# L0 attention: the maxima's bias on VectorE, the exponentials one slot earlier, the projection's bias as a product on TensorE

## The chip, the cores and the metric

The kernel runs on one core of a Trainium2 chip. The metric is the device time of one execution in microseconds. In the profile PE is TensorE, ACT is ScalarE, DVE is VectorE, POOL is GpSimd and SP is SyncE, which issues most of the DMAs. Each of them works through its own instructions in order.

## The reference

The program is a stack of six layers on x of 8 x 512 x 256, all in float32:

```python
x = x + 0.5 * _L0_ffn_ref(_layernorm(x), ...)    # f1: 64 experts, top 3
x = x + _L0_attn_ref(_layernorm(x), ...)         # a1: the layer that is changed
x = x + 0.5 * _L0_ffn_ref(_layernorm(x), ...)    # f2
x = x + 0.5 * _L1_ffn_ref(_layernorm(x), ...)    # f3: 8 experts, top 2
x = x + _L1_attn_ref(_layernorm(x), ...)         # a2
x = x + 0.5 * _L1_ffn_ref(_layernorm(x), ...)    # f4
```

The changed layer, for each batch row of 512 tokens, 16 heads and a window of 32 earlier tokens:

```python
strain = disp_win - disp[:, :, :, None, :]
bond_act = gelu(strain @ w_strain + b_strain + state[:, :, :, None, :] @ w_state_i
                + state_win @ w_state_j + rel_emb @ w_pos)
bond_logits = (bond_act @ w_bond_out)[..., 0] + b_bond_out[0]
damage_act = gelu(strain @ w_damage + b_damage)
damage = sigmoid((damage_act @ w_damage_out)[..., 0] + b_damage_out[0])
logits = where(cmask, bond_logits - damage * 10.0, -inf)
weights = softmax(logits, axis=-1)
out = einsum('bntd,bntde->bnte', weights, val_win)
return out.transpose(0, 2, 1, 3).reshape(Bx, Tx, Cx) @ w_cproj + b_cproj
```

## The kernel before

A batch row is 4 tiles of 128 tokens (`NT`). `l0_attn` cuts the gelus of a batch row into 16 units: 2 groups of 8 heads, 2 halves of the window, and 4 interleaved offsets in each. One unit is 4 offsets x 512 tokens on 128 partitions, once for the bond (tile `ub`) and once for the damage (tile `ud`).

The order of the work is written out by hand. Time is counted in slots, one unit to a slot, 16 slots to a batch row, 8 batch rows. In slot s:

- `unit_add(s)` adds up the arguments of unit s: `ub` by four instructions on DVE (L670), `ud` by one long one on POOL (L676);
- `unit_act(s-1)` runs both gelus of the unit before on ACT (L681);
- then come the evacuations (`later`) of what the steps of slot s-1 left in PSUM;
- `unit_pe(s-2)` reduces the unit before that on PE (L692);
- and last the steps that the list `plan` has for this slot. A step's PE part is issued at once, the function that it returns is run in the next slot.

`ub` and `ud` have three buffers each, so unit s can be added up once PE is done with unit s-3. Four PSUM banks hold the sums of the units, two `bq`, and the two banks of pool `ps` (tile `m`) serve every other product in turn.

The steps of `plan` that matter here, with their slot counted from the batch row's first unit (the steps of later and earlier batch rows share these slots: k and k - 16 or k + 16 coincide):

- 6, 10, 14, 18 `logits`: the tanh of a half on ACT (`th`, L701), then one instruction on DVE (L702);
- 11, 12 and 19, 20 `less_maxima`: PE turns logits into tokens by partitions (L717, L721); in the next slot DVE takes the maximum of each head's window (`mx`, L729), ACT adds the constant `b_bond` to the maxima (L730), and DVE writes logits + `b_bond` - `mx` into `e` (L731). `e` has a single buffer, which holds a whole batch row;
- 22 `exponentials`: one instruction on ACT over all of `e` (L740); 22 `fetch_values`;
- 23, 24 `weights`: DVE sums `e` (L746) and takes the reciprocal, POOL multiplies (L748), and 8 DMAs for each half write the result into a band in DRAM (L753);
- 23 to 34 `fetch_weights`, `turn_weights`: the band is read back and turned; 33, 37 `weigh`: it is multiplied with the values, and ACT copies the result to `o` (L802);
- 39, 41 `project`: `o` times `w_cproj` on PE (L812), and DVE adds it to `x` (L816);
- for the batch row that comes after: -14 `norm`, -13 and -12 `turn` (L558, copied by ACT to `xnT` at L559), -12 `add_bias`, which adds `b_cproj` to the whole `x` of the batch row on POOL (L550), -11 and -10 `means`, -10 to 2 the keys and queries, of which `damage_keys` leaves `dk` on ACT (L657) and `dq` on DVE (L658).

For the first 132 slots each engine keeps exactly this order of issue. The slots after that, the end of the last batch row, are ordered together with the routing of the next layer by the tile framework.

Of the kernel before, what the change touches and what calls it, by code (L numbers as in the profile page):

```python
# [8 lines left out]
F32 = mybir.dt.float32  # L9
I32 = mybir.dt.int32  # L10
U32 = mybir.dt.uint32
AF = mybir.ActivationFunctionType
ALU = mybir.AluOpType
# [4 lines left out]
P = 128  # L18
NB = 8
T = 512  # L20
D = 256
NT = T // P
KC = D // P
# [20 lines left out]
def bcast_rows(ap, n):  # L44

    return bass.AP(tensor=ap.tensor, offset=ap.offset, ap=[[0, n]] + [list(d) for d in ap.ap[1:]])
# [295 lines left out]
def l0_attn(c, w, tag):  # L342
    nc, tc = c.nc, c.tc
    with ExitStack() as ctx:
        dram = ctx.enter_context(tc.tile_pool(name=f"{tag}_dram", bufs=1, space=DRAM))
        const = ctx.enter_context(tc.tile_pool(name=f"{tag}_const", bufs=1))
# [21 lines left out]
        w_cproj = const.tile([P, KC, D], F32, name="w_cproj")  # L368
# [3 lines left out]
            nc.sync.dma_start(b_disp, w["b_disp"].rearrange("o (g p) -> p (o g)", p=P))  # L372
        b_val = const.tile([P, D], F32, name="b_val")
        nc.sync.dma_start(b_val, bcast_rows(w["b_val"], P))
        b_cproj = const.tile([P, D], F32, name="b_cproj")
        nc.sync.dma_start(b_cproj, bcast_rows(w["b_cproj"], P))
        b_bond = const.tile([P, 1], F32, name="b_bond")
        nc.sync.dma_start(b_bond, bcast_rows(w["b_bond_out"], P))
        b_dam = const.tile([P, 1], F32, name="b_dam")
# [159 lines left out]
        def norm(b):  # L539
# [5 lines left out]
            row[b] = {  # L545
                "xn": xn, "xnT": rp.tile([P, KC, T], F32, name="xnT"), "zT": rp.tile([P, KC, T], F32, name="zT")
            }

        def add_bias(b):
            nc.gpsimd.tensor_tensor(  # L550
                c.x[b], c.x[b], b_cproj.unsqueeze(1).to_broadcast([P, NT, D]), ALU.add
            )

        def turn(b, kc):
            xn = row[b]["xn"]
# [151 lines left out]
        def less_maxima(b, g, i2):  # L707
            t = grp[b, g]
            if g == 0 and i2 == 0:
                row[b]["e"] = rp.tile([P, NT, 2, GH, WIN], F32, name="e")  # L710
            tp = ps.tile([P, T], F32, name="m")
            tv = tp.rearrange("p (i h a d) -> p i h a d", i=2, h=GH, a=2)
            for j in range(2):
                i = 2 * i2 + j
                for half in range(2):
                    if i == 0:
                        nc.tensor.matmul(  # L717
                            tv[:, j, :, half, :], lhsT=c.ident, rhs=mask[:, :, 16 * half : 16 * (half + 1)],
                            start=True, stop=False,
                        )  # L720
                    nc.tensor.matmul(  # L721
                        tv[:, j, :, half, :], lhsT=t["lo", half][:, i * P : (i + 1) * P], rhs=place,
                        start=(i > 0), stop=True,
                    )

            def after():
                mx = sp.tile([P, 2, GH], F32, name="mx")
                tw = tp.rearrange("p (i h d) -> p i h d", i=2, h=GH)
                nc.vector.tensor_reduce(out=mx, in_=tw, axis=AX.X, op=ALU.max)  # L729
                nc.scalar.activation(mx, mx, AF.Identity, bias=b_bond)  # L730
                nc.vector.scalar_tensor_tensor(  # L731
                    out=row[b]["e"][:, 2 * i2 : 2 * i2 + 2, g], in0=tw, scalar=b_bond,
                    in1=mx.unsqueeze(3).to_broadcast([P, 2, GH, WIN]), op0=ALU.add, op1=ALU.subtract,
                )

            return after
# [70 lines left out]
        def project(b, i2):  # L807
            o = row[b].pop(("o", i2))
            mm = ps.tile([P, 2, D], F32, name="m")
            for j in range(2):  # L810
                for a in range(KC):
                    nc.tensor.matmul(  # L812
                        mm[:, j, :], lhsT=o[:, j, a, :], rhs=w_cproj[:, a, :], start=(a == 0), stop=(a == KC - 1)
                    )
            xs = c.x[b][:, 2 * i2 : 2 * i2 + 2, :]
            return lambda: nc.vector.tensor_tensor(xs, xs, mm, ALU.add)  # L816


        plan = [
            (-14, norm), (-13, turn, 0), (-12, turn, 1), (-12, add_bias), (-11, means, 0), (-10, means, 1),  # L820
            (-10, disp, 0), (-9, values, 0), (-8, values, 1), (-8, state, 0), (-7, disp, 1), (-6, bond_keys, 0),
            (-5, bond_queries, 0), (-4, damage_keys, 0), (-3, state, 1), (0, bond_keys, 1), (1, bond_queries, 1),
            (2, damage_keys, 1), (6, logits, 0, 0), (10, logits, 0, 1), (11, less_maxima, 0, 0),
            (12, less_maxima, 0, 1), (14, logits, 1, 0), (18, logits, 1, 1), (19, less_maxima, 1, 0),
            (20, less_maxima, 1, 1), (22, exponentials), (22, fetch_values), (23, weights, 0), (24, weights, 1),
            (24, fetch_weights, 0), (24, fetch_weights, 1), (25, fetch_weights, 2), (29, turn_weights, 0, 0),
            (30, turn_weights, 0, 1), (30, turn_weights, 1, 0), (31, fetch_weights, 3), (31, turn_weights, 1, 1),
            (31, turn_weights, 2, 0), (32, turn_weights, 2, 1), (33, weigh, 0), (33, turn_weights, 3, 0),
            (34, turn_weights, 3, 1), (37, weigh, 1), (39, project, 0), (41, project, 1),
        ]  # L830
        slots = {}
# [1090 lines left out]
def macaron_kernel(ctx, tc, x, l0a, l0f, l1a, l1f, out):  # L1922
# [10 lines left out]
    with ExitStack() as k0:  # L1933
        k0_ = l0_consts(c, l0f, k0.enter_context(c.tc.tile_pool(name="l0_const", bufs=1, side="right")))
        c.zero = k0_.zero
        f1, f2 = (l0_ffn(c, l0f, tag, k0_, l0_dram) for tag in ("f1", "f2"))
        a1 = l0_attn(c, l0a, "a1")
        next(a1)
        with c.tc.tile_pool(name="f1_w", bufs=5) as wp:
            f1.route(2, lambda: next(a1))  # L1940
            next(a1)
            f1.experts(wp)
        next(a1)
        f2.route(1)
        next(a1, None)
        consts, load = l1_ffn_consts(c, l1f, ctx.enter_context(c.tc.tile_pool(name="f_const", bufs=1)))
        with c.tc.tile_pool(name="f2_w", bufs=5) as wp:
            f2.experts(wp, load)
# [176 lines left out]
```

## Time and profile before

| what | value |
|---|---|
| time, median of 3 runs | 3248.82 us (3236.14 to 3258.5) |
| the profiled execution | 3218.18 us, of which the span is 3216.4 us |
| PE, PEld, DVE, ACT, POOL busy in the span | 87%, 62%, 50%, 51%, 52% |
| mean granted TensorE clock | 0.92 |
| busy in 640 to 1313 us: PE, DVE, ACT, POOL | 559.33, 491.10, 592.68, 573.11 of 673 us |
| gelus L681 (`ub`, `ud`), 128 each | 1920 and 1914 ns |
| `ud` on POOL L676, 128 | 4195 ns |
| `ub` on DVE L670, 512 | 738 ns |
| maxima's bias on ACT L730, 32 | 305 ns |
| projection's bias on POOL L550, 8 | 2368 ns |
| exponentials on ACT L740, 8 | 1913 ns |
| table loads on ACT, each | 1283 ns |

The shares of the whole span are means over six layers with different limits. L0 attention has the stretch from about 650 to 1400 us; in its steady part, the 128 slots, a batch row repeats nearly the same timeline. A line of the timeline has the start, the duration, the engine, the line of the source, the operation, the tiles it writes and reads, the shape and a count; in brackets it has the idle time before it and what ended that. A count over 1 means several instructions in a row, and the duration is theirs together.

### The profile page before, as it was taken

The page shows a single profiled execution, that of the slowest core. Times are in us where ns is not written, and L with a number is a line of the kernel's source. Part 1 is how long each engine was busy: PE and PEld are TensorE (multiplying, and loading weights), DVE is VectorE, ACT ScalarE, POOL GpSimd, SP SyncE. Part 2 cuts the span into 40 slices and gives each one's busy share as a digit, 9 for nine tenths or more (in the row PEclk, how much of TensorE's full clock was granted, in tenths as well). Part 3 has the DMA queues.
Part 4 walks back from the last instruction along what each step waited for, and adds up shares of the span by engine and source line. Part 5 has one row for each costly group of instructions (what it writes and reads, how often), then busy time and mean ns, then how long its engine had stood idle before and what let it go on. Part 6 is the DMA issues. An engine that isn't in the chain of part 4 may idle for free. (4 is left out here: it accounts for less than half of the span.)

```text
span 3216.4 us, 53865 instructions
## 1 busy us (share of the span) xinstructions
PE 2784.4 (87%) x20353; PEld 1997.6 (62%) x20353; DVE 1593.0 (50%) x3773; ACT 1641.3 (51%) x2608; POOL 1658.6 (52%) x1298
## 2 busy tenths in 40 slices
PE   6699999978888888778999997787899999998783
PEld 6688888833334343467888896575455555554662
DVE  7511111167777777672111113675657666573564
ACT  4133333369999999632333333266444535434452
POOL 3344444368888888524444442255535454324565
PEclk9799999988999999788999997799889989898897
DMA  7599999531555666786999994144101010001355
GB/s 232 192 304 306 306 302 307 171 104 10 78 85 85 84 85 88 84 240 215 307 308 304 303 307 132 40 141 130 29 15 41 28 35 27 20 7 58 109 172 162
DMA packets 378178, 478.66 MB, mean 149 GB/s; under 512 B 93080, under 2 KB 339872, under 8 KB 361536
## 3 DMA queue, kind: packets, MB, share of 16 engines
q1 hardware_dynamic: 339376, 403.50, 44.3%
q0 software_dynamic: 38544, 71.73, 9.5%
q8 instruction: 161, 2.64, 0.3%
q14 instruction: 97, 0.79, 0.1%
HBM read 382.21 MB, written 88.47 MB: 146 GB/s over the span
## 5 line engine op out<-in xcount | busy, mean ns | idle before, releaser
L316 ACT ACTIVATE hT<-hp,b1T 128x128 f32<-128x128 f32 x1024 | 376.0, 368 | 612.7 <-PE hp L312 580.2
L312 PE MATMUL hp<-xeT,w 128*128 128x128 f32 x4096 | 561.8, 280 | 23.6 <-DVE xeT L305 22.5
L312 PEld LDWEIGHTS hp<-xeT,w 128*128 128x128 f32 x4096 | 527.9, 193 | 68.8 <-DVE xeT L305 30.2
L676 POOL TENSOR_TENSOR ud<-dk,dq 128x2048 f32<-128x2048 f32 x128 | 533.4, 4195 | 58.3 <-PE do L692 33.8
L319 PE MATMUL yp<-w,hT 128*128 128x256 f32 x2048 | 506.6, 380 | 0.0
L321 DVE TENSOR_TENSOR y<-yp,b 128x256 f32<-128x256 f32 x128 | 54.3, 425 | 839.0 <-PE yp L319 538.4
L319 PEld LDWEIGHTS yp<-w,hT 128*128 128x128 f32 x2048 | 360.1, 191 | 32.9
L670 DVE SCALAR_TENSOR_TENSOR ub<-bk,relb,bq 128x512 f32<-128x512 f32 x512 | 345.0, 738 | 6.7 <-PE bo L692 6.1
L1804 ACT ACTIVATE pt<-s 128x1024 f32<-128x1024 f32 (+3 forms) x256 | 180.2, 705 | 295.6 <-PE s L1800 233.8
L681 ACT ACTIVATE ud<-ud 128x2048 f32<-128x2048 f32 x128 | 245.0, 1914 | 24.3 <-POOL ud L676 24.1
L295 POOL PARTITION_BROADCAST b<-b2r x128 | 82.2, 646 | 338.7 <-DVE y L321 318.1
L681 ACT ACTIVATE ub<-ub 128x2048 f32<-128x2048 f32 x128 | 245.7, 1920 | 6.7 <-DVE ub L670 6.6
L1737 POOL TENSOR_SCALAR_AFFINE_SELECT d<-d 128x512 f32<-128x512 f32 x128 | 84.6, 661 | 315.6 <-DVE d L1727 315.0
L297 POOL DMA_INDIRECT xe<-f_xn_d,slots x128 | 128.8, 1006 | 216.4 <-PE xp L303 176.5
L323 POOL DMA_INDIRECT f_acc_d<-y,slots x128 | 205.3, 1604 | 60.6 <-DVE y L322 31.6
L1338 POOL DMA_INDIRECT xe<-f_xn,f_tok x156 | 149.7, 959 | 147.2 <-PE tp L1357 73.2
L1727 DVE TENSOR_TENSOR d<-s,fac 128x320 f32<-128x320 f32 (+1 forms) x256 | 120.2, 470 | 210.5 <-PE s L1715 178.7
L1769 POOL TENSOR_TENSOR d<-d,nm 128x640 f32<-128x640 f32 (+1 forms) x128 | 154.7, 1214 | 65.9 <-DVE nm L1749 65.7
L1788 PE MATMUL s<-qm,kp 32*128 32x384 f32 (+2 forms) x768 | 146.3, 458 | 19.7 <-ACT pt L1804 11.0
L1390 ACT COPY we<-wall 128x768 f32 x156 | 129.6, 832 | 47.7 <-DVE xeT L1360 18.5
L692 PE MATMUL bo<-ub,o_w_bond_out 128*32 128x512 f32 x1024 | 145.1, 638 | 9.5 <-ACT ub L681 9.5
L1710 PE MATMUL s<-kp,qp 32*128 32x160 f32 (+1 forms) x1024 | 145.1, 366 | 4.5 <-DVE mx L1732 2.0
(500 smaller groups left out, 5146.6 us busy)
## 6 DMA issues: line engine op xcount, KB each, us to landing
w<-in_L_ffn_w_dram SPq DMA_DIRECT2D x256, 1024.0 KB
vb<-val_d SPq DMA_DIRECT2D x16, 1024.0 KB
pb<-band_d SPq DMA_DIRECT2D x32, 512.0 KB
f_y<-y SPq DMA_DIRECT2D x117, 128.0 KB
f_xn_d<-xn SPq DMA_DIRECT2D x16, 512.0 KB
f_acc_d<-x SPq DMA_DIRECT2D x16, 512.0 KB
x<-f_acc_d SPq DMA_DIRECT2D x16, 512.0 KB
val_d<-vhalf SPq DMA_DIRECT2D x16, 512.0 KB
```

Source lines behind the costliest of these rows:

```text
L312: nc.tensor.matmul(hp[:, jj, :], lhsT=w1[:, kc, :].rearrange("c (j p) -> c j p", j=NJ0)[:, j, :], rhs=xeT[:, kc, :], start=(kc == 0), stop ...
L316: nc.scalar.activation(hT[:, j, :], hp[:, jj, :], AF.Gelu, bias=b1T[:, j, e : e + 1])
L319: nc.tensor.matmul(yp, lhsT=hT[:, j, :], rhs=w2[:, j, :], start=(j == 0), stop=(j == NJ0 - 1))
L323: nc.gpsimd.indirect_dma_start(out=acc_d[:, :], out_offset=bass.IndirectOffsetOnAxis(ap=slots[:, e : e + 1], axis=0), in_=y, in_offset=Non ...
L670: nc.vector.scalar_tensor_tensor(out=ub[:, j, :], in0=bk[:, d : d + T], scalar=relb[:, d : d + 1], in1=t["bq"], op0=ALU.add, op1=ALU.add,)
L676: nc.gpsimd.tensor_tensor(ud, win, t["dq"].unsqueeze(1).to_broadcast([P, 4, T]), ALU.subtract)
L681: nc.scalar.activation(m, m, AF.Gelu)
L692: nc.tensor.matmul(out[32 * j : 32 * (j + 1), :], lhsT=outw[name][:, k, :], rhs=m[:, j, :], start=(k == 0), stop=(k == 3),)
L1338: nc.gpsimd.indirect_dma_start(out=xe[n], out_offset=None, in_=xn_d[h][:, :], in_offset=bass.IndirectOffsetOnAxis(ap=part_of[h]["tok_i"][: ...
L1769: nc.gpsimd.tensor_tensor(d[:, i, :, lo:], d[:, i, :, lo:], pads["nm"][n % 2][:, i, :, x : x + 1].to_broadcast([P, 4, NEAR - lo]), ALU.add,)
L1788: nc.tensor.matmul(tile_[:, j, P:w_], lhsT=pads["k"][g][r, kb * P : (kb + 1) * P], rhs=grp[n]["qm"][r, (kb + 1) * P :], start=True, stop=True,
L1804: nc.scalar.activation(grp[n]["pt"][:, 2 * pair : 2 * pair + 2, :w_], tile_[:, :, :w_], AF.Exp)
```

## The change

Three edits. The bias that is added to the 128 x 16 maxima moves from an ACT instruction to a DVE instruction with the same operands. The step `exponentials` moves from slot 22 to slot 21, the slot in which the last subtraction (of `less_maxima` at slot 20) is issued. And `b_cproj` is no longer spread over 128 partitions and added to `x` on POOL: it is loaded as one row, and PE adds it as a third product into each accumulation of `project`, a row of ones times `b_cproj`.

```diff
-        b_cproj = const.tile([P, D], F32, name="b_cproj")
-        nc.sync.dma_start(b_cproj, bcast_rows(w["b_cproj"], P))
+        b_cproj = const.tile([1, D], F32, name="b_cproj")
+        nc.sync.dma_start(b_cproj, w["b_cproj"])
...
-        def add_bias(b):
-            nc.gpsimd.tensor_tensor(
-                c.x[b], c.x[b], b_cproj.unsqueeze(1).to_broadcast([P, NT, D]), ALU.add
-            )
...
                 nc.vector.tensor_reduce(out=mx, in_=tw, axis=AX.X, op=ALU.max)
-                nc.scalar.activation(mx, mx, AF.Identity, bias=b_bond)
+                nc.vector.tensor_scalar(mx, mx, b_bond, None, ALU.add)
...
                     nc.tensor.matmul(
-                        mm[:, j, :], lhsT=o[:, j, a, :], rhs=w_cproj[:, a, :], start=(a == 0), stop=(a == KC - 1)
+                        mm[:, j, :], lhsT=o[:, j, a, :], rhs=w_cproj[:, a, :], start=(a == 0), stop=False
                     )
+                nc.tensor.matmul(mm[:, j, :], lhsT=c.ones_row, rhs=b_cproj, start=False, stop=True)
...
-            (-14, norm), (-13, turn, 0), (-12, turn, 1), (-12, add_bias), (-11, means, 0), (-10, means, 1),
+            (-14, norm), (-13, turn, 0), (-12, turn, 1), (-11, means, 0), (-10, means, 1),
...
-            (20, less_maxima, 1, 1), (22, exponentials), (22, fetch_values), (23, weights, 0), (24, weights, 1),
+            (20, less_maxima, 1, 1), (21, exponentials), (22, fetch_values), (23, weights, 0), (24, weights, 1),
```

`c.ones_row` is a tile of ones of 1 x 128 that `setup` has made already.

## The prediction

> **What bounds the kernel now.** I read the busy time by stretch first, because the change lies in one stage only, L0 attention, which runs from 650 to about 1400 us. Its steady part is 128 slots of one unit each.
>
> ```profile
> core 0: us, PE busy (x) PEld busy (x) DVE busy (x) ACT busy (x) POOL busy (x), PEclk, DMA share, GB/s
> ...
> 1000.00:1100.00 100.00, 85.82 (x903) 40.15 (x900) 72.26 (x116) 93.86 (x81) 89.33 (x24) 1.00 0.51 70
> ```
>
> ACT (93.86 of 100) and POOL (89.33) are both nearly full, DVE is not. From one exponential to the next (1031.47, 1113.66, 1195.63 in the trace) a batch row costs 82.2 us. Next come the waits on ACT in the stage (total, times, longest):
>
> ```profile
> ACT ud L681 <- POOL ud L676: 24.1, 16, 2.7
> ACT mx L730 <- DVE mx L729: 22.1, 16, 3.3
> ```
>
> Then the timeline of one row, engine by engine. Slots 12 and 13:
>
> ```profile
> 1065.39 0.75 DVE L731 SCALAR_TENSOR_TENSOR e<-m,b_bond,mx 128x512 f32<-128x512 f32 x1 [3.22 <-ACT ub L681]
> ...
> 1069.40 0.31 ACT L730 ACTIVATE mx<-mx,b_bond 128x16 f32<-128x16 f32 x1 [2.35 <-DVE mx L729]
> ...
> 1069.41 3.81 POOL L676 TENSOR_TENSOR ud<-dk,dq 128x2048 f32<-128x2048 f32 x1 [0.34 <-PE do L692]
> ```
>
> The subtraction at 1065.39 is late in each row after the first: 17 to 18 us after POOL's second product e*rs of the row before (1047.97 here), when the 16 DMAs out of the single buffer e have landed. So the row is a ring: e*rs on POOL, DMAs, subtraction, ub(13) on DVE, ACT's gelus 13 to 21, exponential, th, DVE's th, ub(23) and sums, e*rs again. ACT's 3.3 us of waits for ud lie inside the slack before that subtraction and cost nothing. Slots 19 to 22 of the same row:
>
> ```profile
> 1098.34 0.73 ACT L657 ACTIVATE dk<-m,rep 128x512 f32<-128x512 f32 x1
> ...
> 1113.66 1.92 ACT L740 ACTIVATE e<-e 128x2048 f32<-128x2048 f32 x1
> 1115.48 0.67 ACT L701 ACTIVATE th<-do,b_dam 128x512 f32<-128x512 f32 x1
> ...
> 1102.41 0.68 DVE L729 TENSOR_REDUCE mx<-m 128x16 f32<-128x512 f32 x1
> 1103.47 0.75 DVE L731 SCALAR_TENSOR_TENSOR e<-m,b_bond,mx 128x512 f32<-128x512 f32 x1 [0.38 <-ACT mx L730]
> ...
> 1101.33 2.38 POOL L550 TENSOR_TENSOR x<-x,b_cproj 128x1024 f32<-128x1024 f32 x1
> 1103.65 8.37 POOL L676 TENSOR_TENSOR ud<-dk,dq 128x2048 f32<-128x2048 f32 x2
> 1113.40 3.81 POOL L676 TENSOR_TENSOR ud<-dk,dq 128x2048 f32<-128x2048 f32 x1 [1.39 <-PE do L692]
> ```
>
> Below I count from dk at 1098.34: reduction +4.07, th +17.14.
>
> **The maxima's bias on DVE.** ACT loses 32 instructions of 0.31 us, each 0.21 of issue, and their waits. DVE gains 32 in place, 128x16, SBUF to SBUF, with a pointer scalar. The nearest free row (128x8, pointer scalar, L438) takes 0.23. But POOL runs nearly always here, and these rows show what such an instruction does beside it:
>
> ```profile
> 2028.42 2.34 POOL L1050 TENSOR_TENSOR x<-x,bs 128x1024 f32<-128x1024 f32 x1 [7.54 <-DVE rank L1187]
> ...
> 2028.80 1.99 DVE L1191 TENSOR_SCALAR ts<-ts 128x16 f32<-128x16 f32 x1
> ...
> 2885.23 0.63 POOL L1737 TENSOR_SCALAR_AFFINE_SELECT d<-d 128x512 f32<-128x512 f32 x1 [2.16 <-DVE d L1727]
> 2885.34 0.55 DVE L1311 TENSOR_SCALAR behind<-iota,part 128x39 f32<-128x39 f32 x1
> ```
>
> L1191, the same operation on the same shape, takes 1.99 us and ends 0.03 us after POOL's instruction; it takes 0.18 at its median. L1311 has a pointer scalar and also ends with POOL's (2885.89 against 2885.86). So each new instruction waits for the POOL instruction in progress. Two rules stand against each other here. The Trainium skill's ScalarE: Activation LUTs (Rules for kernel authors) puts an add on VectorE; by that the new instruction costs its 0.23. Its SBUF — State Buffer (Who interferes with whom) says a tensor_scalar in a 2-port mode and a GpSimd instruction exclude each other for a whole instruction. By the first the sum is the rival "free" below, +1 us; by the second, with the two rows behind it, +67. I take the rows. ud takes 3.81 us for two units in four (1113.40) and 4.56 for the others (8.37 - 3.81).
>
> *Slot 20.* POOL's ud(21) no longer stands behind the bias add. It waits for PE's unit 18, which ends at 1102.42, and POOL starts 0.18 after such an end: +4.26. The reduction ends at +4.75 and the new instruction wants to start at +4.79: POOL is 0.53 ahead. ud(21) ends at +8.82; the bias ends at +9.07, the subtraction runs from +9.11 to +9.86 (before +5.13). Behind it on DVE stand ub(21) and the next reduction, +12.40 to +13.08.
>
> *Slot 21.* Pool "m" has two banks. Slot 20's product of the maxima takes the one that ACT's xnT frees (PE starts it at 1103.96, 0.05 after that copy), so the next row's second turn is left with the one that the subtraction reads, and PE waits until +9.92. It takes 0.53, unit 19 behind it 1.93, and with 0.18 ud(22) starts at +12.56. The new instruction wants +13.12 and is 0.56 late again. ud(22) ends at +16.37, the bias at +16.63, the subtraction at +17.42.
>
> **The exponential in slot 21.** On ACT it now follows gelu(20) and waits for that subtraction: load at +17.47, exponential +18.76 to +20.67, gelu's table +20.69 to +21.97, gelu(21) 3.62, the copy of o 0.46, th at +26.1. Before, it was at +17.14: **+9.0 us a row.** Two table loads a row remain, but gelu's now lies before th and not behind it, 1.30 of the 9.0. The reader might expect earlier weights; there are none, as DVE's sums in slot 23 stand behind th of slot 22 in DVE's order, and POOL's e*rs behind them. From th on all is as before. On the load's price the same ScalarE page (What ACT_TABLE_LOAD costs) has 2.66 us for a switch, 1.28 of load and 1.38 of drain; here the load starts 0.02 after the copy (1111.78 + 0.57, 1112.37) and the exponential 0.01 after the load. By the page the row would be 1.4 longer, 10 us over seven; I take the trace. Seven rows have these slots in the steady part: 7 x 9.0 = 63.
>
> *Slots 12 and 13.* In slot 12 the new instruction waits for ud(12), to about 1064.6, before the DMA's 1065.39: nothing. In slot 13 ACT no longer waits for the reduction. dk and then ub(13) on DVE (done 1068.76) are late next, so gelu(13) starts at 1068.84 and not 1070.19: -1.35. But the new instruction wants 1069.41, and ud(14) starts at 1069.41. If POOL is first, it waits 3.8, dq and ub(14) with it and PE's turn and state behind that bank; state, th and gelu(14) come at 1078.0 and not 1075.41: +2.6. I see no reason for either: +0.6 a row, 7 rows 4.4, less 0.9 in row 0, which has no DMA to wait for.
>
> **The projection's bias.** POOL loses 8 x 2.36 us at nothing gained: in that stretch ACT waits for no ud, and POOL already idles 1.39 for PE. PE gains 2 products of one partition for each project, 4 instructions at 0.23 (8 take 1.84 between L812 and L617), 0.92 twice a row. Behind them on PE stands unit 22, whose result ud(25) needs only 4.4 us later; were that cover gone, 8 x 1.84 = 15 us. In the tail +0.9, less 0.5 for the shorter chain of maxima. The vector's load is one DMA at 68 us, far ahead.
>
> **Sum:** 63 + 3.5 + 0.4 = +67 us. On the profiled execution (3218.18; span 3216.4 and 1.8 around it) that is 3285; that execution lies 30.6 below the median shown, so on the median 3315.
>
> **Rivals.**
> 1. *Free* (chance 0.16): the new instruction takes 0.23 beside POOL. Then the subtraction is 0.14 earlier, the exponential waits until +9.96, th comes 1.5 later, and slot 13 gives 1.35 back: +0.15 a row, 3250, not slower. For it: the form with this pointer at 128x16 is in no row. Against: L1191, L1311.
> 2. *Once* (0.16): slot 21's instruction slips in ahead of ud(22), as 0.56 us is little. Slots 20 to 22 cost 5.7 a row, so +44: 3293.
> 3. *More* (0.18): slot 13 always loses (+18 for all rows against 3.5), or in slot 12 a ud back to back takes its turn first, +3.9 a row: +81 to +94, 3330 to 3343.
>
> **Numbers.** The forecast holds 0.5. The range runs from just below "once" to above "more", 3265 to 3350, and leaves out "free". A change of 1% (32 us) is about what a measurement can tell from none. Slower by more: 0.5 + 0.18 + most of "once", 0.8; within 1%: 0.17; faster 0.03, since even without collisions the gain ends at 1.35 a row, some 10 us.
>
> **What would show it.** Right: the new instruction on DVE with a mean of 2 to 3 us, ending with a POOL ud; exponentials some 91 us apart; ACT idle before the exponential by about 6 us, on DVE e; POOL idle before ud(22), on PE. Wrong: the new instruction at 0.2 to 0.3 us throughout, or rows still 82 us apart.

## The result, and the profile after

| | median of its runs | runs | profiled execution | its span | granted clock |
|---|---|---|---|---|---|
| before | 3249.3 us | 3236.1 to 3258.5 | 3218.18 us | 3216.4 us | 0.920 |
| after | 3300.2 us | 3274.2 to 3313.5 | 3293.21 us | 3291.5 us | 0.907 |

The changed kernel is slower: ratio 1.0148, 95% interval 1.011 to 1.0186, that is 48 us (36 to 60), from four runs of each. The forecast was 3315 in a range of 3265 to 3350; direction and size hold, but two of its terms do not, and they cancel in part.

First the stage. In the profiled executions L0 attention (up to the first DMA of expert weights for the stage behind it) ends at 1403.03 us before and at 1460.54 after, 57.5 us later; 2.9 of these were there at the stage's first gelu (675.8 and 678.6). The other 17.6 us of the difference lie in the stages behind it, which the change doesn't touch; before's execution also had the higher clock there (0.90 against 0.89). The same stretch by engine, after:

```profile
core 0: us, PE busy (x) PEld busy (x) DVE busy (x) ACT busy (x) POOL busy (x), PEclk, DMA share, GB/s
1000.00:1100.00 100.00, 83.07 (x736) 38.70 (x734) 77.31 (x110) 82.31 (x63) 77.12 (x20) 0.97 0.63 83
```

ACT fell from 93.86 to 82.31 and POOL from 89.33 to 77.12: both now wait more. DVE rose from 72.26 to 77.31. PEclk, 1.00 before, is 0.97; that turns out to matter. What ACT waits for in the stage (total, times, longest):

```profile
ACT ud L676 <- POOL ud L671: 25.4, 16, 2.7
ACT state L628 <- PE m L623: 21.3, 14, 4.5
...
ACT xnT L554 <- PE m L553: 12.4, 7, 2.4
...
ACT pt L772 <- PE m L766: 10.8, 4, 2.7
ACT e L735 <- DVE e L726: 8.5, 7, 1.3
```

The 22.1 us of waits for the maxima are gone and the wait for ud is as large as before (24.1), but the waits for PE (state, xnT, pt) and for the subtraction e are new or larger: before, state had 5.5, xnT 0.5, and pt and e none. The cause is in the group of the new instruction (duration min/median/max in ns):

```profile
L725 DVE TENSOR_SCALAR mx<-mx,b_bond x32: 226/1816/4035, 739.7 to 1394.9; 128x16 f32<-128x16 f32 x32
```

An instruction whose shortest run is 0.23 us takes 1.82 at its median and 4.04 at most. The 32 take 57.6 us together, a mean of 1.80. Slot by slot in one row: slots 12 and 13,

```profile
1002.08 2.22 DVE L725 TENSOR_SCALAR mx<-mx,b_bond 128x16 f32<-128x16 f32 x1
1006.22 0.75 DVE L726 SCALAR_TENSOR_TENSOR e<-m,b_bond,mx 128x512 f32<-128x512 f32 x1 [1.92 <-DMA pb<-band_d]
...
1010.23 3.85 DVE L725 TENSOR_SCALAR mx<-mx,b_bond 128x16 f32<-128x16 f32 x1
...
1010.24 3.81 POOL L671 TENSOR_TENSOR ud<-dk,dq 128x2048 f32<-128x2048 f32 x1 [0.90 <-PE do L687]
...
1014.97 1.09 PE L766 MATMUL m<-ident,pb 128*128 128x128 f32 x4 [4.91 <-issue]
1015.85 2.85 PE L623 MATMUL m<-zT,w_state 128*128 128x512 f32 x4
...
1018.74 0.69 ACT L628 ACTIVATE state<-m,rep 128x512 f32<-128x512 f32 x1 [2.06 <-PE m L623]
```

In slot 12 the wait is harmless, since the DMA is later still. In slot 13 the instruction and POOL's product begin within 0.01 us of each other and end together (1014.08 and 1014.05). Behind it wait the subtraction, the bank that PE's turn needs, and ACT's state. Slots 19 to 22, counted from dk at 1042.83:

```profile
1047.59 4.04 DVE L725 TENSOR_SCALAR mx<-mx,b_bond 128x16 f32<-128x16 f32 x1
...
1055.67 0.23 DVE L725 TENSOR_SCALAR mx<-mx,b_bond 128x16 f32<-128x16 f32 x1
...
1047.07 4.52 POOL L671 TENSOR_TENSOR ud<-dk,dq 128x2048 f32<-128x2048 f32 x1 [1.22 <-PE do L687]
1056.50 3.81 POOL L671 TENSOR_TENSOR ud<-dk,dq 128x2048 f32<-128x2048 f32 x1 [4.92 <-PE do L687]
...
1053.62 0.58 ACT L554 COPY xnT<-m 128x512 f32<-128x512 f32 x1 [2.40 <-PE m L553]
1054.22 1.28 ACT L735 ACT_TABLE_LOAD   x1
1056.73 1.92 ACT L735 ACTIVATE e<-e 128x2048 f32<-128x2048 f32 x1 [1.23 <-DVE e L726]
...
1064.04 0.69 ACT L696 ACTIVATE th<-do,b_dam 128x512 f32<-128x512 f32 x1
...
1052.47 1.11 PE L553 MATMUL m<-ident,xn 128*128 128x128 f32 x4 [3.65 <-DVE e L726]
1053.51 1.94 PE L687 MATMUL bo<-ub,o_w_bond_out 128*32 128x512 f32 x8
```

Slot 20's instruction is blocked for the rest of POOL's product (4.04, to 1051.63; the product ends at 1051.59). Slot 21's isn't blocked: it runs at 1055.67, 0.83 us ahead of POOL. The table load runs at 1054.22, before the exponential's wait is over. th comes 21.21 us after dk, against 17.14.

### The profile page after: what moved, and what is told of

It is laid out like the page before. It is cut to its first block, busy times and chain, and to the rows that moved or that the text cites. A ratio compares the mean times of both kernels' runs of the same rounds, so it can differ in the third digit from the quotient of the medians.

```text
span 3291.5 us, 53959 instructions
## 1 busy us (share of the span) xinstructions
PE 2842.5 (86%) x20417; PEld 2027.6 (62%) x20417; DVE 1644.9 (50%) x3805; ACT 1638.9 (50%) x2578; POOL 1641.6 (50%) x1290
## 5 line engine op out<-in xcount | busy, mean ns | idle before, releaser
L312 PE MATMUL hp<-xeT,w 128*128 128x128 f32 x4096 | 561.9, 280 | 23.6 <-DVE xeT L305 22.5
L295 POOL PARTITION_BROADCAST b<-b2r x128 | 82.3, 647 | 334.4 <-DVE y L321 299.4
```

The source lines that it names most:

```text
L312: nc.tensor.matmul(hp[:, jj, :], lhsT=w1[:, kc, :].rearrange("c (j p) -> c j p", j=NJ0)[:, j, :], rhs=xeT[:, kc, :], start=(kc == 0), stop ...
```

## The experiments

The kernels of the experiments ran in three groups, each beside the kernel before on the same chip. That kernel took 3227, 3265 and 3284 us in them, so only ratios within a group are compared. In the table, "late" is the time from dk of slot 19 to th of slot 22, "slots 12 to 14" that from the subtraction of slot 12 to th of slot 14, and "transfers" that from the end of POOL's second e*rs to the subtraction of slot 12: each measured in six rows of the profiled execution, from the timeline, with the median where no range stands. All other parts of a row have nearly the same length in every kernel: over six rows together they differ from before's by 3 us at most.

| kernel | ratio to before (95%) | late | slots 12 to 14 | transfers |
|---|---|---|---|---|
| before | 1 | 17.14 | 9.45 | 17.5 |
| all three, first | 1.0148 (1.011 to 1.0186) | 21.21 | 8.4 to 13.9 | 19.8 |
| maxima only | 1.0038 (1.0016 to 1.006) | 16.75 | 8.3 to 13.9 | 17.6 |
| exponentials only | 1.0024 (1.0002 to 1.0046) | 18.54 | 9.45 | 17.9 |
| projection only | 1.0027 (1.0004 to 1.0049) | 17.13 | 9.45 | 17.8 |
| PSUM source | 0.9982 (0.9961 to 1.0003) | 17.49 | 8.3 to 10.0 | 17.5 |
| before, no bias | 0.9949 (0.993 to 0.9969) | 16.09 | 8.08 | 17.7 |
| maxima + exponentials | 1.006 (1.0037 to 1.0082) | 18.06 | 8.4 to 13.9 | 18.0 |
| maxima + projection | 1.0065 (1.0041 to 1.0089) | 19.62 | 9.05 | 18.5 |
| POOL's product split | 1.0137 (1.0094 to 1.0181) | 20.29 | 8.4 to 11.4 | 17.7 |
| exponentials + projection | 1.004 (1.0017 to 1.0064) | 18.54 | 9.45 | 19.8 |
| all three, again | 1.0126 (1.0071 to 1.0182) | 21.22 | 9.7 to 13.9 | 20.0 |
| after, no bias | 0.9963 (0.994 to 0.9987) | 17.49 | 8.08 | 20.5 |
| no bias + projection | 0.9946 (0.9923 to 0.9969) | 16.09 | 8.09 | 20.4 |

The last column says what not to explain: the four kernels of the last group (the last four rows of the table) all need about 20 us there, with the bias of the maxima on VectorE or on ScalarE or gone; the eight of the first two groups need 17.5 to 18.5 at their medians. So a longer stretch of transfers does not need the change. Before's profiled execution had the short one (17.5) and after's the long one (19.8); summed over six rows that is 14.1 of the 50.7 us between their profiles. It is left out of the account of the change below.

### Maxima only

```diff
-                nc.scalar.activation(mx, mx, AF.Identity, bias=b_bond)
+                nc.vector.tensor_scalar(mx, mx, b_bond, None, ALU.add)
```

> The kernel before with the maxima's bias on VectorE as its only edit (exponentials in slot 22, the projection's bias on POOL). Theory LOCK (the new instruction waits for POOL's instruction in progress, and hurts where something urgent stands behind it): the instruction takes 1 to 2.5 us on average, up to 4; slot 13 costs as in the changed kernel, 3.65 us where the tie is lost and -1.35 where it is won, about +10 us in all; in slots 20 and 21 the exponential of slot 22 has room for a late subtraction, so 0 to 3 us a row. Sum +10 to +30: 3260 to 3280. Theory MOVE (the earlier exponentials alone are what costs): no change, 3249 within 8, or a gain of 10. Theory PRODUCT (the bias's products on TensorE cost): no change as well.

It gave +12 us, at the low end of LOCK. The instruction takes 0.69 at its median and up to 6.87. Slot 13 is lost in three of the six rows (13.3 to 13.9 in place of 9.45) and won by about 1.1 in two. In slots 20 and 21, where POOL's bias add still stands, it costs nothing in five of six rows. The longest wait shows that the instruction can wait for more than one of POOL's:

```profile
966.93 21.12 POOL L676 TENSOR_TENSOR ud<-dk,dq 128x2048 f32<-128x2048 f32 x5
...
981.22 6.87 DVE L730 TENSOR_SCALAR mx<-mx,b_bond 128x16 f32<-128x16 f32 x1
```

Five products ran back to back until 988.05; the instruction asked at 981.22, did not get in where one product ended and the next began, and ended at 988.09, 0.04 after the last.

### Exponentials only

```diff
-            (20, less_maxima, 1, 1), (22, exponentials), (22, fetch_values), (23, weights, 0), (24, weights, 1),
+            (20, less_maxima, 1, 1), (21, exponentials), (22, fetch_values), (23, weights, 0), (24, weights, 1),
```

> The kernel before with the exponentials in slot 21 as its only edit (the maxima's bias stays on ScalarE). LOCK: the subtraction of slot 21 ends about 10.2 us after dk, the table load covers the rest, the exponential does not wait; gelu's table load now lies before th, 1.3 us a row: +9 us, 3258 within 8. MOVE: nearly the whole loss, +40 to +55, about 3295. PRODUCT: no change.

It gave +8 us; the late part is 1.40 longer in each row, the 1.30 that gelu's table load takes ahead of th. No row has an exponential that waits. MOVE falls: the earlier slot is worth a sixth of the loss, not the whole.

### Projection only

The bias product on TensorE and no add on POOL, as in the change, and nothing else.

> The kernel before with the projection's bias as a product on TensorE as its only edit, POOL's add removed. LOCK: POOL idles instead, 3249 within 8. MOVE: the same. PRODUCT: +40 or more.

It gave +9 us (1 to 16), while its late part and slots 12 to 14 stay as before; in six rows together, without transfers, it is 2.4 us longer, all of it one row. So the profile shows no place for 9 us, and the interval reaches down to 1.0004. PRODUCT falls as the cause of the loss.

### The same instruction, from PSUM

```diff
-                nc.vector.tensor_scalar(mx, mx, b_bond, None, ALU.add)
+                spare = sp.tile([P, 2, GH], F32, name="spare")
+                nc.vector.tensor_scalar(spare, tw[:, :, :, 0], b_bond, None, ALU.add)
-                nc.vector.scalar_tensor_tensor(
-                    out=row[b]["e"][:, 2 * i2 : 2 * i2 + 2, g], in0=tw, scalar=b_bond,
-                    in1=mx.unsqueeze(3).to_broadcast([P, 2, GH, WIN]), op0=ALU.add, op1=ALU.subtract,
+                nc.vector.tensor_tensor(
+                    row[b]["e"][:, 2 * i2 : 2 * i2 + 2, g], tw, mx.unsqueeze(3).to_broadcast([P, 2, GH, WIN]),
+                    ALU.subtract,
                 )
```

> The changed kernel with its VectorE bias instruction replaced by one of the same operation, shape and scalar pointer that reads PSUM (a column of the product) and writes a spare tile nobody reads; the subtraction then takes the maxima without the bias from the product without the bias, which is the same difference. VectorE so has as many instructions in the same places, but none that goes from SBUF to SBUF there. LOCK: the instruction takes 0.2 to 0.3 us everywhere, rows are 82 to 84 us apart, slot 13 no longer waits: 3240 to 3262. MOVE and PRODUCT, and a theory that one more VectorE instruction in the chain costs by its place: 3290 to 3305 as in the changed kernel.

This is the run that decides between the theories. Operation, shape, scalar pointer, place and count are as in the changed kernel, as are the exponentials' slot and the product on TensorE; the operand comes from PSUM. Two things change with it: the operand is now one column in 32 of the product and not a dense tile, and the subtraction has one operation less. No run separates the source from the column's step.

```profile
L726 DVE TENSOR_SCALAR spare<-m,b_bond x32: 215/222/226, 733.6 to 1335.7; 128x16 f32<-128x16 f32 x32
```

All 32 take 0.22 us, the longest 0.226. The whole loss is gone (0.9982), and rows are 82.3 apart. The Trainium skill's SBUF — State Buffer (Who interferes with whom) gives a reason: a tensor_scalar in a 2-port mode and a GpSimd instruction exclude each other for a whole instruction. With 57.6 us against 7.1 for these 32 instructions this case agrees; which port they wait for, no trace shows.

### Before, without the bias

```diff
-                nc.scalar.activation(mx, mx, AF.Identity, bias=b_bond)
-                nc.vector.scalar_tensor_tensor(
-                    out=row[b]["e"][:, 2 * i2 : 2 * i2 + 2, g], in0=tw, scalar=b_bond,
-                    in1=mx.unsqueeze(3).to_broadcast([P, 2, GH, WIN]), op0=ALU.add, op1=ALU.subtract,
+                nc.vector.tensor_tensor(
+                    row[b]["e"][:, 2 * i2 : 2 * i2 + 2, g], tw, mx.unsqueeze(3).to_broadcast([P, 2, GH, WIN]),
+                    ALU.subtract,
                 )
```

> The kernel before without any bias on the maxima: the subtraction takes the maxima of the product from the product, which is the same difference; exponentials in slot 22 and the bias add on POOL as before. ScalarE loses 32 instructions of 0.31 us and its waits for the maxima, VectorE gains none. LOCK, with the row's ring as the prediction has it: slot 13's gelu starts 1.35 us earlier a row, the rest is slack: -5 to -14 us, ratio 0.996 to 0.9985. If those waits of ScalarE were slack altogether: 1.000.

It is faster than before by 0.5% (17 us of 3265, interval 10 to 23), more than the 5 to 14 us that were expected, and both its parts are those of the ring: slots 12 to 14 get 1.37 us a row shorter (8.08 for 9.45), the late part 1.05. Most of the 1.05 is what ACT's own bias instructions cost there, which the expectation had called slack: a wait of 0.46 for the maxima, and twice 0.21 of issue (0.88). Before:

```profile
1103.13 0.31 ACT L730 ACTIVATE mx<-mx,b_bond 128x16 f32<-128x16 f32 x1 [0.46 <-DVE mx L729]
```

Without the bias, slots 19 to 22 on ACT stand without a wait:

```profile
1088.98 0.61 ACT L559 COPY xnT<-m 128x512 f32<-128x512 f32 x1
...
1093.05 0.63 ACT L559 COPY xnT<-m 128x512 f32<-128x512 f32 x1
...
1100.90 0.67 ACT L701 ACTIVATE th<-do,b_dam 128x512 f32<-128x512 f32 x1
```

### Maxima and exponentials

The changed kernel with POOL's bias add put back: which of the other two edits turns the lock into time?

> The changed kernel with the projection's bias back on POOL (bias of the maxima on VectorE, exponentials in slot 21). POOL's first product of slot 20 stands behind the bias add again. LOCK: in slot 20 the new instruction then waits only for the end of the add, 0.5 to 1.7 us as with the maxima's bias alone, and not 4.0; the subtraction of slot 21, for which the exponential waits, comes 1 to 2 us late: alone-costs of the two edits (12 and 8) and 5 to 12 more, +25 to +32, ratio 1.008 to 1.010. If the exponential's slot is what turns the lock into time, whatever POOL does: +45 to +50 as with all three edits, ratio 1.014 or more.

+20 us, the sum of the two edits alone (12 and 8), and under the 25 to 32 that LOCK gave. With the add back in slot 20, the maxima's instruction asks while the add runs, and gets in between the add and the product:

```profile
1021.86 2.40 POOL L550 TENSOR_TENSOR x<-x,b_cproj 128x1024 f32<-128x1024 f32 x1
1024.20 8.38 POOL L676 TENSOR_TENSOR ud<-dk,dq 128x2048 f32<-128x2048 f32 x2
...
1023.66 0.64 DVE L730 TENSOR_SCALAR mx<-mx,b_bond 128x16 f32<-128x16 f32 x1
```

The 2.38 us of POOL's add that the change removes had been what kept the long product away from that instruction.

### Maxima and projection

The changed kernel with the exponentials back in slot 22.

> The changed kernel with the exponentials back in slot 22 (bias of the maxima on VectorE, projection's bias on TensorE). LOCK: slot 20 is blocked by 4.0 us in nearly every row, as with all three edits; the exponential of slot 22 has room for the late subtraction, but TensorE's second turn still waits for its bank, so ScalarE's copy of xnT comes about 2.4 us late: 7 x 2.4 and the costs of the maxima's bias alone (12) and of the product alone (0 to 9): +27 to +38, ratio 1.008 to 1.012. If the early exponential is what turns the lock into time: +12 to +20, ratio 1.004 to 1.006.

+21 us (13 to 29): between the two theories' figures, and again the sum of the two edits alone (12 and 9). Slot 20 is blocked for 4.03 in five rows, as with all three edits, yet the exponential does not wait; only the copy of xnT and a ub do:

```profile
1028.29 0.59 ACT L554 COPY xnT<-m 128x512 f32<-128x512 f32 x1 [2.40 <-PE m L553]
1029.81 1.91 ACT L676 ACTIVATE ub<-ub 128x2048 f32<-128x2048 f32 x1 [0.93 <-DVE ub L665]
...
1035.31 1.91 ACT L735 ACTIVATE e<-e 128x2048 f32<-128x2048 f32 x1
```

2.40 + 0.93 - 0.88 (ACT's own bias copies are gone) is 2.45; the late part is 2.48 longer. Slot 13 waits only 0.98 in these rows, so this kernel gains 0.4 there where the changed one loses 3.6 or more.

### POOL's product in two halves

```diff
...
-            nc.gpsimd.tensor_tensor(ud, win, t["dq"].unsqueeze(1).to_broadcast([P, 4, T]), ALU.subtract)
+            for h in range(2):
...
+                nc.gpsimd.tensor_tensor(
+                    ud[:, 2 * h : 2 * h + 2, :], win, t["dq"].unsqueeze(1).to_broadcast([P, 2, T]), ALU.subtract
+                )
```

> The changed kernel with each of POOL's ud products of 128x2048 issued as two of 128x1024. LOCK, if VectorE gets its turn where a POOL instruction ends: the new instruction's longest wait falls from 4.0 to about 2 us, slot 20's to 1.4 to 2; slots 20 to 22 cost some 2 us a row in place of 4, slot 13's lost tie 1.9 in place of 3.65: ratio 1.005 to 1.010. LOCK, if POOL's next instruction takes its turn first when it stands ready: still up to 4 us, ratio 1.014 to 1.018. If the length of POOL's instruction does not matter: no change against the changed kernel, about 1.015, with the same 4.0 us.

The length of POOL's instruction sets the wait: slot 20's falls from 4.03 to 1.86 in five rows, where the instruction gets in between the halves. But it need not get in. Once it waited for the rest of one half and four more, until a row of halves that ran back to back was through (1279.29 + 15.24 = 1294.53; the line has the last seven of them):

```profile
1279.29 15.24 POOL L674 TENSOR_TENSOR ud<-dk,dq 128x1024 f32<-128x1024 f32 x7
...
1285.24 9.33 DVE L730 TENSOR_SCALAR mx<-mx,b_bond 128x16 f32<-128x16 f32 x1
```

And slot 21's instruction, free in the changed kernel, waits 1.5 in four rows. So the late part falls by only 0.9 at its median, and the one long wait makes 26.5 of it in its row; the ratio (1.0137, from six runs) can't be told from the changed kernel's. Neither form of LOCK that was written down holds by itself. In the six profiles with the bias on VectorE from SBUF (the changed kernel is in them twice), a waiting instruction met 88 boundaries at which POOL's next instruction follows at once (within 0.05 us): it got in at 80 and was passed over at 8, in five waits. What decides it is open.

### Exponentials and projection, and all three again

> The kernel before with the exponentials in slot 21 and the projection's bias on TensorE (the maxima's bias stays on ScalarE). If the loss needs the bias of the maxima on VectorE as well: the sum of the two edits alone, 8 + 9 = +17, ratio 1.003 to 1.007, rows 83 to 85 us apart. If an earlier exponential and a free POOL in slot 20 are enough: +40 or more, ratio above 1.012.

> The changed kernel once more, beside the other runs of this call, for the sum: the three edits alone give 12 + 8 + 9 = 29 us, the two pairs with the maxima's bias on VectorE gave the sums of their parts (20 and 21). If all three together are more than their sum, ratio 1.013 to 1.017; if the runs of the first result were high by chance, 1.009.

Without the maxima on VectorE the other two give 1.004, no more than their sum (1.0051), with the late part of the exponentials alone (18.54); its rows are 86 us apart, not 83 to 85, since the transfers are longer in this group. All three again give 1.0126, just under the 1.013 to 1.017 that was expected, with the same late part as the first time (21.22) and slot 13 lost four times. The edits alone add up to 1.0089, and half the sum of the three pairs is 1.0083 (0.0060 + 0.0065 + 0.0040, halved). All three together gave 1.0148 and 1.0126. The second interval alone does not exclude the sum; the rows say where the excess is. Over six rows without transfers the first execution is 36.6 us longer than before and the second 39.4, while the edits alone are 12.8, 8.4 and 2.4 longer (23.6). The excess already stands in one pair: the late part of maxima and projection is 11.6 us longer over the six rows, while these edits alone make 1.6 and nothing of it. In that pair's time it doesn't show, because its slot 13 is 3.0 us shorter, where the maxima alone lose 10.5. So a pair's time can equal the sum of its edits although they act on each other.

### Without the bias in the changed kernel, and with the product alone

> The changed kernel without the bias on the maxima, which the subtraction doesn't need (it takes the maxima of the product from the product); exponentials in slot 21, projection's bias on TensorE. LOCK: as the kernel whose instruction read PSUM, less 0.22 us a slot on VectorE: ratio 0.996 to 1.000. If the place of the exponential costs its 1.3 us of table load a row, it stays above the kernel before without the bias (0.995) by some 9 us.

> The kernel before without the bias on the maxima, exponentials in slot 22, and the projection's bias on TensorE. LOCK: no VectorE instruction waits for POOL and th of slot 22 stands before gelu's table load; the product alone cost 0 to 9 us: ratio 0.995 to 0.999, at or just above the kernel before without the bias (0.995). If POOL's time freed in slot 20 is worth something once the bias is gone: 0.992 to 0.995.

After without the bias is at 0.9963; with the exponentials back in slot 22 it is at 0.9946. The late parts differ by 1.40 (17.49 and 16.09), the table load again, while the two ratios' intervals overlap. The product on TensorE shows no effect either way: 0.9946 (0.9923 to 0.9969) with it, 0.9949 (0.993 to 0.9969) without it, so the two cases of the last expectation can't be told apart. These two kernels beat both the kernel before and the changed one; the simpler of them is the kernel before with the bias dropped from both sides of the subtraction.

## Why the prediction was right, and where it wasn't

**The lock (right).** It took the two rows of the trace over the rule that an add belongs on VectorE. The mean is 1.80 us, a little under the 2 to 3 that it said. Twenty of the 32 took longer than 0.3 us, and each of them ends 0.03 to 0.04 us after an instruction of POOL; so do all 131 such ones in the six profiles that have it on VectorE from SBUF (the changed kernel is in them twice). On ScalarE the same bias took 0.31: that rule cost time here (12 us with the maxima's bias alone).

**Slot 20 (right).** Said: the instruction is late by 0.53 and is done at +9.07, the subtraction at +9.86. Measured: late by 0.52 (1047.59 against 1047.07), done at +8.80, the subtraction at +9.58, in five rows of seven. That removing POOL's add causes this was in the working; the pair without the removal shows it.

**Slot 21 (wrong; the rival "once").** Said: ud(22) at +12.56, the instruction late by 0.56. Measured: ud(22) at +13.67, the instruction at +12.84, 0.83 ahead. The failed step is "It takes 0.53, unit 19 behind it 1.93": these are durations at full clock. PE's wait for its bank lasted 3.65 us, and then its turn took 1.11 and the first half of the unit 1.94, where it takes 1.06 in slot 20. The granted clock (the third number from the end) shows it:

```profile
core 0: us, PE busy (x) PEld busy (x) DVE busy (x) ACT busy (x) POOL busy (x), PEclk, DMA share, GB/s
1051.00:1052.00 1.00, 0.00 (x0) 0.00 (x0) 0.96 (x2) 0.21 (x1) 0.59 (x1) 0.97 0.00 0
1052.00:1053.00 1.00, 0.53 (x3) 0.54 (x4) 1.00 (x3) 0.00 (x0) 0.00 (x0) 0.50 0.00 0
...
1055.00:1056.00 1.00, 1.00 (x12) 0.30 (x8) 0.93 (x4) 0.50 (x1) 0.00 (x0) 0.83 0.00 0
1056.00:1057.00 1.00, 1.00 (x103) 0.86 (x98) 1.00 (x2) 0.27 (x1) 0.50 (x1) 1.00 0.00 0
```

Half speed from about 1052 until between 1055 and 1056, some 3.4 us; it began some 3 us after PE's last product (1048.82). The Trainium skill's TensorE: Matmul & The Clock Gate (What's actually happening) has this rule: after an idle window of about 3.4 us the clock halves, until TensorE was busy for about as long. The times here come near to that.

That the clock decides slot 21 can be seen in the kernel with POOL's product split. In four of its rows PE waits only 1.48 us for the bank, the clock is 1.00, ud(22) starts 0.52 us ahead of the instruction (the prediction had 0.56), and the instruction waits:

```profile
1029.06 0.66 PE L553 MATMUL m<-ident,xn 128*128 128x128 f32 x4 [1.48 <-DVE e L731]
1029.65 1.07 PE L692 MATMUL bo<-ub,o_w_bond_out 128*32 128x512 f32 x8
...
1031.75 3.95 POOL L674 TENSOR_TENSOR ud<-dk,dq 128x1024 f32<-128x1024 f32 x2 [1.22 <-PE do L692]
1032.27 1.51 DVE L730 TENSOR_SCALAR mx<-mx,b_bond 128x16 f32<-128x16 f32 x1
```

In another of its rows the clock is 0.50 in the same place, the first half of the unit takes 1.94, and the instruction runs in 0.23 us, 1.12 ahead of POOL. There, too, the idle time was only 1.48 us, from which the page's rule does not give a halved clock; why it fell in that row is open.

The prediction's own figures implied some 3 us of idle time (from +6.78 to +9.92), and it didn't ask what that does to the next products. The idle time was 3.65 because slot 20's product also began earlier, at +4.83 and not at the +5.62 of before's trace, since xnT no longer stands behind ACT's bias. Before, and then after:

```profile
1103.96 1.16 PE L721 MATMUL m<-place,th 128*128 128x128 f32 x8 [1.53 <-ACT xnT L559]
```

```profile
1047.66 1.16 PE L716 MATMUL m<-place,th 128*128 128x128 f32 x8 [0.77 <-ACT xnT L554]
```

Either point would have moved the choice towards "once".

**The exponential (mis-sized).** Said: +9.0 us a row, of which 1.30 is gelu's load ahead of th. Measured: +4.07 in five rows of seven, and +1.5 and +1.1 in the first and the last. Besides slot 21's block there is a second error, the load placed behind the wait ("waits for that subtraction: load at +17.47"): the load ran at 1054.22, as soon as ACT was free, and lay inside the wait for e (of 2.5 us between the copy and the exponential, 1.28 is load and 1.23 idle). The late part adds up: xnT's wait for PE 2.40, the wait for e 1.23, gelu's load ahead of th 1.30, less 0.88 for ACT's own bias copies, is 4.05; measured 4.07. The experiments show the terms one at a time: 1.40 with the exponentials alone, 2.48 with maxima and projection. Summed over six rows: 21.4 us, where 9.0 a row would be 54.

**Slot 13 (mis-sized the other way).** Said: a tie, +0.6 a row between -1.35 and +2.6. Measured in six rows: lost four times at +3.6 to +4.4, won once at -1.06, once +0.28; together +15.3, 2.5 a row. Three kernels of pairs or single edits lost the tie three times in six or not at all, so its outcome is not settled by the edit itself. A lost tie costs more than 2.6 for the same reason as above: PE idles 4.91 behind it, and its four products for state then take 2.85 us (1.98 before), for most of it at a granted clock of 0.50.

**The projection (right on the late part).** No gain on POOL, nothing on PE's unit 22: the late part is 17.13 with it alone. That it cost 9 us (1 to 16) has no place in the profile and stays open.

**The sum.** Said +67: 63 in the late part, 3.5 in slot 13. Measured in six rows 21.4 and 15.3, 36.7 together; with 3.2 up to the end of row 0, of which 2.9 stood before the first gelu and are hardly the change's, and at most 3.5 after the sixth row, where transfers are in it, some 37 to 43. The ratio says 48 (36 to 60). So the first term was two and a half times too large, the second four times too small, and that the sum came within 20 us is in part luck. What ran is the rival "once" in slot 21 together with most of "more" in slot 13; the median of 3300 lies nearer to the 3293 of "once" than to the 3315 of the forecast. Of the signs that were named, POOL's idle time before ud(22) on PE came (4.92), the exponentials of the first seven rows stood 87 to 94 us apart (about 91 said), and the 6 us of ACT's idle time before the exponential did not come (1.23).

## What to carry to other kernels

Before a small SBUF-to-SBUF instruction goes to VectorE, look at what POOL runs at that moment and at what stands behind the instruction in VectorE's order: here 0.31 us on ScalarE became up to 6.9 us (9.3 with POOL's products split), and reading the operand from PSUM or dropping the bias by algebra cured it. Work that is removed from an engine moves its next instruction forward, possibly into a collision; removing 2.4 us of add from POOL did that. When a predicted wait makes TensorE idle for some 3.5 us or more, price what follows it at half clock: in the changed kernel, from 700 to 1400 us, all 16 such idle times were followed by a clock of 0.50 to 0.66 (over the first half microsecond). It is no sharp limit, for in other kernels here 4.07 us were followed by 1.00 and 1.48 us by 0.50. And try edits alone and in pairs, and compare their rows part by part, before giving a loss to one of them.

## What the runs showed of the hardware that was not expected

- A VectorE instruction that waits for POOL's is not sure of a turn when POOL's ends: it got in between add and product (0.64 us) or between two halves (1.86), and it was passed over (6.87 us across one boundary, 9.33 across four).
- An ACT_TABLE_LOAD runs before the wait of the ACTIVATE that needs it is over: in the first seven rows of the changed kernel it was done before the operand came. In the row shown it started at 1054.22, the operand came at 1056.70 (VectorE's subtraction ends there).
- TensorE ran at a granted 0.50 for some 3 us after 3.65 us of idle time, in the middle of a stretch (1000 to 1100 us) whose mean is 0.97.
- The 16 transfers of a row and the load behind them took some 2 us more in the last group (19.8 to 20.5) than in the first two (17.5 to 18.5), for every kernel.
